# A hand-written list scheduler: longer planned load latency, a two-instruction LSTM cell, unbroken sums and an earlier rank for two batches

## The chip, the cores and the metric

The kernel runs on one core of one Trainium2 chip. The metric is the device time in microseconds, and the number that counts is the median of several executions. One further execution was profiled; its rows give start and duration of every instruction on the five engines: PE (TensorE, with PEld for its weight loads), DVE (VectorE), ACT (ScalarE), POOL (GpSimd) and SP (which here only issues DMAs).

## The reference, cut to what matters

There are 32 graphs ("batches") of 512 nodes with 128 features each, and an adjacency matrix of 512 x 512 of zeros and ones per graph. Four layers follow each other, each as `x = x + layer(relu(layernorm(x)), adj)`:

```
layer 0   attention:  q, k, v = relu(h Wq), relu(h Wk), relu(h Wv);  x += softmax(masked q k^T) v
layer 1   dyn  = conv1d(last 128 nodes of h)           # 32 x 128 steps x 128
          lw   = lstm(dyn)                             # 128 steps, for 32 graphs at once
          x   += sigmoid((D^-1/2 (A + I) D^-1/2 h) lw)
layer 2   four sublayers, each: tanh of (normalised A times projected nodes) + own projection
layer 3   x += prelu(A (h W^T) + bias)

lstm step:  z = dyn_t W_ih + b + h W_hh;   i, f, g, o = split(z)
            c = sigmoid(f) c + sigmoid(i) tanh(g);   h = sigmoid(o) tanh(c)
```

The LSTM needs only the last 128 nodes of each graph, but of all 32 graphs, so layer 0 must have been done for those nodes everywhere before step 0. Layer 1's result needs the LSTM's last state for every graph.

## The kernel before, in words

The fast path, `symmetric`, has four parts.

*Pass 1* (`pass_1`) does, for each batch, layer 0 for the last 128 nodes and the convolution, and stores keys, values and the normalised input in DRAM.

*The recurrence* (`lstm`) has 128 steps. A step is one block of small products on PE (L1216, tiles of 32 columns, "tiled"), a tanh of three gates on ACT (L1242), the cell on DVE (L1249 to L1251), a tanh of the fourth gate (L1257) and of the cell (L1259) on ACT, and the new state with its transpose on DVE (L1263, L1264). The transpose releases the next step's products. The sigmoids are written as tanh of half the argument, which is why the cell reads "(tanh + 1) times".

*Pass 2* (`pass_2`) does layer 0 for the other 384 nodes: it loads what pass 1 stored and the adjacency (L1284 to L1297), computes the query product (L1299), the scores (L1308), the exponentials times mask (L1311, L1312) and the weighted values (L1317), all with 32-column tiles on PE. `squares` (L1356) turns the adjacency into the type that PE takes and sums its rows, on ACT. For the first 24 batches (`EARLY`) it also does layer 1's sum over neighbours, `sums_of_1`, whose matmuls are in `aggregate` (L1403): two halves (high and low part of the values) of four matmuls 128x512 with 128x128 weights, each half an operation of its own. The updated x goes to DRAM (L1328), the sums too (L1344).

*The last stage* (`rest`) finishes layers 1 to 3 batch by batch: gates (L1452), the comparison of the adjacency with its transpose by two scans per batch on DVE (L1471), four sublayers (L1498 projection, L1385 and L1386 split into two parts, L1403 sum, L1505 scaling, L1509 own projection, L1513 tanh) and layer 3. It begins with batches 26 and 27 (`FIRST`).

All of these only record operations. `Plan.run` then decides the order on each engine: it simulates the engines with a duration given for each operation, a hop between engines, and for a DMA a `gap`, the extra time from the end of its issue slot to its landing (2.0 us if nothing else is said; the slot of 1024 KB is 0.1 + 1024/315 us). At each moment it takes the operation that can start first, and among those that can start at once the one of lowest rank. The LSTM steps have ranks 0 to 127, which are urgent: an operation that isn't urgent is passed over when it would still run, by more than 0.15 us, at the time at which the next urgent one is expected on its engine. Pass 1 has ranks from 10,000, pass 2 from 20,000, the last stage from 30,000; ranks of the last stage are recomputed from how much work lies behind an operation. The last four batches of pass 2 rank among the last stage. The order that comes out is fixed in the program: each engine executes its list in order and waits on semaphores, so an operation whose data come late holds all that stands behind it on its engine.

Buffers are named by tags with counts (`BUFS`); the whole adjacency has two buffers (`a`), the transformed one six (`ar`).

## Time and profile before

| | |
|---|---|
| median of 3 runs | 1316.08 us (1315.48 to 1326.4) |
| the profiled execution | 1324.53 us, span of its instructions 1322.7 us |
| PE, PEld busy | 1274.2 us (96%), 977.1 us (74%) |
| DVE, ACT, POOL busy | 990.9 us (75%), 847.3 us (64%), 392.8 us (30%) |
| first products of the recurrence, last transpose | about 182 us, about 515 us |
| mean DMA rate | 177 GB/s |

The shares are means over stages of different kinds. The stage from 182 to 515 us is the recurrence with pass 2 beside it; up to about 195 us pass 1 overlaps it; from 515 us the last stage runs alone, with what pass 2 has left. In a row of the profile, "x16" counts hardware instructions, of which one product in 32-bit floats takes two.

### The profile page before, as it was taken

Reading aid. Unit: us, or ns where it says so; the run is one execution under the profiler, and the core shown is the slowest. Engines: PE = TensorE matmul, PEld = TensorE weight load, DVE = VectorE, ACT = ScalarE, POOL = GpSimd, SP = SyncE. Lnnn points to the kernel's source line nnn. Section 1 sums busy time; section 2 is a strip of 40 time slices with the busy share of each in tenths; the row PEclk is TensorE's granted clock in tenths of the full one; section 3 lists DMA queues with packets and bytes.
Section 4 is the critical chain, followed back from the end, with each engine's and each line's share of the span. In section 5 each row is a group of like instructions: output and inputs, shape, how many; then the busy total and the mean of one; then the engine's idle time right before and its main releaser. Section 6 shows DMA issues by size and latency. Waiting matters only on the chain.

```text
span 1322.7 us, 32990 instructions
## 1 busy us (share of the span) xinstructions
PE 1274.2 (96%) x12098; PEld 977.1 (74%) x12099; DVE 990.9 (75%) x3392; ACT 847.3 (64%) x2116; POOL 392.8 (30%) x737
## 2 busy tenths in 40 slices
PE   9999999988988999799999999999999999999996
PEld 6888866656666667577787877778787787787774
DVE  7998878867868887766777767767677777787644
ACT  5666767666777665575666666666676676676423
POOL 4655432213213214422231322313223132242100
PEclk9999999999999999899999999999999999999999
DMA  8888888757757657895667766776767754673311
GB/s 259 261 284 276 266 292 260 238 170 225 230 185 238 202 164 217 194 211 145 158 142 159 165 156 160 158 152 161 154 163 160 166 124 88 151 170 71 48 33 35
DMA packets 300587, 234.52 MB, mean 177 GB/s; under 512 B 138240, under 2 KB 244480, under 8 KB 300416
## 3 DMA queue, kind: packets, MB, share of 16 engines
q1 hardware_dynamic: 283520, 215.54, 58.3%
q0 software_dynamic: 16896, 16.78, 8.1%
q8 instruction: 98, 1.61, 0.5%
q14 instruction: 73, 0.60, 0.2%
HBM read 138.16 MB, written 62.65 MB: 152 GB/s over the span
## 4 chain that ended last, share of the span: by engine, by line
PE 84%; DMA 5%; DVE 5%; ACT 2%; issue 2%; POOL 1%; SPq 1%; ACTq 0%; POOLq 0%; DVEq 0%
PE f_pa L1403 18%; PE f_py L1498 15%; PE f_pa L1509 15%; PE f_pg L1403 8%; PE f_s L1308 5%; PE f_po L1317 4%; PE f_z L1216 3%; DMA f_a<-in_adj_dram 3%; PE f_p L1550 2%; PE f_pl L1452 2%; PE f_pk L1123 2%; PE f_pv L1139 2%; PE f_sl L1156 2%; PE f_pol L1166 2%; PE f_pq L1299 1%
## 5 line engine op out<-in xcount | busy, mean ns | idle before, releaser
L1403 PE MATMUL f_pa<-f_ar,f_y 128*128 128x512 f32 x1024 | 300.5, 430 | 5.3 <-DVE f_y L1386 4.5
L1403 PEld LDWEIGHTS f_pa<-f_ar,f_y 128*128 128x128 f32 x1024 | 190.1, 189 | 80.5 <-issue 40.2
L1498 PE MATMUL f_py<-f_wf,f_n 128*128 128x128 f32 x1280 | 174.6, 275 | 0.8 <-ACT f_n L1513 0.8
L1498 PEld LDWEIGHTS f_py<-f_wf,f_n 128*128 128x128 f32 x1280 | 165.5, 192 | 11.2 <-ACT f_n L1513 1.9
L1509 PE MATMUL f_pa<-f_n,f_wf 128*128 128x512 f32 x320 | 152.8, 592 | 0.0
L1356 ACT ACTIVATE f_ar<-f_a 128x512 fp32r<-128x512 f32 x224 | 138.6, 621 | 19.5 <-DMA f_a<-in_adj_dram 18.3
L1513 ACT ACTIVATE f_n<-f_pa,f_bcol 128x512 f32<-128x512 f32 x128 | 88.3, 690 | 92.1 <-PE f_pa L1509 91.7
L1385 ACT CAST f_y<-f_py 128x512 fp32r<-128x512 f32 x128 | 75.0, 586 | 101.0 <-PE f_py L1498 98.7
L1466 POOL DMA_DIRECT2D f_das<-f_ar x32 | 26.9, 839 | 366.5 <-ACT f_ar L1356 313.4
L1317 PE MATMUL f_po<-f_v,f_e 128*32 128x129 f32 x3072 | 108.5, 277 | 8.3 <-issue 6.1
L1505 DVE TENSOR_TENSOR f_pa<-f_pa,f_inv 128x512 f32<-128x512 f32 x128 | 86.7, 693 | 30.6 <-PE f_pa L1403 30.2
L1317 PEld LDWEIGHTS f_po<-f_v,f_e 128*32 128x32 f32 x3072 | 91.0, 111 | 20.8 <-issue 10.4
L1386 DVE TENSOR_TENSOR f_y<-f_py,f_y 128x512 fp32r<-128x512 f32 x128 | 87.6, 685 | 22.7 <-ACT f_y L1385 22.6
L1308 PE MATMUL f_s<-f_q,f_k 128*32 128x384 f32 x1024 | 99.8, 488 | 0.1
L1216 PE MATMUL f_z<-f_w,f_seq 128*32 128x128 f32 x2040 | 83.2, 276 | 16.0 <-DVE f_seq L1264 8.1
L1216 PEld LDWEIGHTS f_z<-f_w,f_seq 128*32 128x32 f32 x2040 | 54.9, 109 | 56.0 <-issue 13.8
L1509 PEld LDWEIGHTS f_pa<-f_n,f_wf 128*128 128x128 f32 x320 | 57.5, 190 | 44.9 <-issue 37.6
L1471 DVE SCALAR_TENSOR_TENSOR f_junk<-f_a,f_aT 128x1024 bf16<-128x1024 f32 x64 | 78.1, 1220 | 5.5 <-DMA f_aT<-f_das 4.3
L1403 PE MATMUL f_pg<-f_ar,f_xp_d 128*128 128x512 f32 x256 | 74.4, 413 | 0.3 <-DVE f_xp_d L1394 0.2
L1498 PE MATMUL f_py<-f_wf,f_T_c 128*128 128x128 f32 x448 | 72.9, 275 | 0.0
L1078 DVE COPY f_hl_d<-f_n 128x1024 uint16<-128x1024 uint16 x28 | 19.4, 693 | 71.2 <-ACT f_n L1513 71.2
L1403 PE MATMUL f_pg<-f_ar,f_xp_c 128*128 128x512 f32 x256 | 71.9, 413 | 0.7 <-ACT f_x L856 0.7
(204 smaller groups left out, 2775.1 us busy)
## 6 DMA issues: line engine op xcount, KB each, us to landing
f_a<-in_adj_dram SPq DMA_DIRECT2D x56, 1024.0 KB
f_das<-f_ar POOLq DMA_DIRECT2D x32, 512.0 KB, 4.8
f_dkq<-f_kh SPq DMA_DIRECT2D x32, 448.0 KB
f_dv<-f_v SPq DMA_DIRECT2D x32, 258.0 KB
f_v<-f_dv SPq DMA_DIRECT2D x32, 258.0 KB
f_x<-in_x_dram SPq DMA_DIRECT2D x32, 256.0 KB
f_al<-in_adj_dram SPq DMA_DIRECT2D x32, 256.0 KB
f_k<-f_dkq SPq DMA_DIRECT2D x32, 256.0 KB
```

The source lines that it names most:

```text
L1216: nc.tensor.matmul(z.t[part, k, :, :], h, w[:, m : m + 4, part], start=False, stop=True, skip_group_check=True)
L1308: PE(R, t_mm(NR), lambda s=s, j=j: quarters(lambda p: nc.tensor.matmul(s.t[p], keys.t[:, j * P + p.start : j * P + p.stop], q.t, start=Tru ...
L1317: PE(R, t_mm(P), lambda t=t, j=j: quarters(lambda p: nc.tensor.matmul(po.t[p, t, :], es[j].t[:, t * P + p.start : t * P + p.stop], v.t[:, ...
L1356: ACT(rank, 0.62, lambda t=t: nc.scalar.activation(ar.t[:, t, :], a.t[:, t, :], AF.Square, accum_out=deg.t[:, t : t + 1]), [a], [(ar, t), ...
L1385: ACT(rank, t_act(N), lambda: nc.scalar.copy(parts.t[:, :, 0, :], src.t), [src], [(parts, 0)])
L1386: DVE(rank, t_dve(N), lambda: nc.vector.tensor_sub(parts.t[:, :, 1, :], src.t, f32(parts.t[:, :, 0, :])), [src, (parts, 0)], [(parts, 1)])
L1403: nc.tensor.matmul(pg.t, parts.t[:, j, k, :], ar.t[:, j, :], start=(k == 0 and j == 0), stop=(k == 1 and j == NT - 1))
L1471: nc.vector.scalar_tensor_tensor(junk, flat(a.t[:, 2 * k : 2 * k + 2, :]), 1.0, flat(aT.t[:, 2 * k : 2 * k + 2, :]), OP.mult, OP.not_equal ...
L1498: nc.tensor.matmul(py.t[:, j, :], nodes[n].t[:, bass.ts(j, P)], wf[:, W_F[i] + c, 0, :], start=False, stop=(c == nch - 1), skip_group_chec ...
L1505: before = DVE(R, t_dve(N), lambda pa=pa: nc.vector.tensor_mul(pa.t, pa.t, inv_row.t), [inv_row], [pa])
L1509: nc.tensor.matmul(pa.t, wf[:, W_F[i] + c, 1, :], nodes[n].t, start=False, stop=(c == nch - 1), skip_group_check=True)
L1513: ACT(R, 0.57, lambda pa=pa, n=n, i=i: nc.scalar.activation(n.t, pa.t, AF.Tanh, bias=bcol[:, i : i + 1]), [pa], [n])
```

## The change

It has four parts.

- *Loads.* The six loads of a batch in pass 2 get `gap=LANDED`, 3.8 us, in place of 2.0. Nothing about the transfers themselves is different; only the planner's idea of when they land.
- *Cell.* The cell state is no longer a tile of its own. It is written into slot 3 of the next step's gate tile, which gets five slots of 32: i, f, g, c, o. One instruction over two slots computes (i + 1) g and (f + 1) c; a second adds half of the latter. Before there were three instructions. The planner's duration goes from 0.43 to 0.30.
- *Unbroken sums.* For ranks below 30,000 `aggregate` is one operation of eight matmuls instead of two of four. It waits for both parts of the values, and it may overrun the next urgent operation by 1.3 us (`patience`), where the rest keeps 0.15.
- *Rank.* The first two batches of the last stage (all of their operations except the transposed copy, its scans, and what has its own rank) are ranked 9,950 lower, among pass 2.

```diff
@@ class Plan
+        self.soon = 0.0
...
+        o.patience = 0.15
...
-                o.rank = self.last + 12 * k - 9 * max(0, k - 28) + 200.0 - (min(behind[o], 60) if sub == 5 else behind[o] + (70 if sub == 2 else 0.0))
+                soon = self.soon if k < 2 and sub < 2 else 0.0
+                o.rank = self.last - soon + 12 * k - 9 * max(0, k - 28) + 200.0 - (min(behind[o], 60) if sub == 5 else behind[o] + (70 if sub == 2 else 0.0))
...
-                    elif held is not None and s < held < s + o.engines[e][0] - 0.15:
+                    elif held is not None and s < held < s + o.engines[e][0] - o.patience:
                         continue
...
+    SOON = 9_950.0
+    LANDED = 3.8
+    PATIENCE = 1.3
+    plan_rest = 30_000
@@ lstm
-            th = new("th", (P, 4, TURN), f"f_th_{t}")
+            th, after_th = after_th or new("th", (P, 5, TURN), f"f_th_{t}"), new("th", (P, 5, TURN), f"f_th_{t + 1}")
...
-            cn = new("c", (P, TURN), f"f_c_{t}")
+            cn = after_th
...
-                    nc.vector.scalar_tensor_tensor(u.t, th.t[:, 1, :], 1.0, c.t, OP.add, OP.mult)
-                    nc.vector.scalar_tensor_tensor(v.t, th.t[:, 0, :], 1.0, th.t[:, 2, :], OP.add, OP.mult)
-                    nc.vector.scalar_tensor_tensor(cn.t, u.t, 0.5, v.t, OP.mult, OP.add)
-                DVE(R, 0.43, cell, [(th, 0), c], [u, v, cn])
+                    nc.vector.scalar_tensor_tensor(uv.t, th.t[:, 0:2, :], 1.0, th.t[:, 2:4, :], OP.add, OP.mult)
+                    nc.vector.scalar_tensor_tensor(cn.t[:, 3, :], uv.t[:, 1, :], 0.5, uv.t[:, 0, :], OP.mult, OP.add)
+                DVE(R, 0.3, cell, [(th, 0), (th, 2)], [uv, (cn, 2)])
...
@@ pass_2 (all six loads alike)
-        DMA(R, 192, lambda: nc.sync.dma_start(hT.t, dkq.t[:, N:]), [dkq], [hT])
+        DMA(R, 192, lambda: nc.sync.dma_start(hT.t, dkq.t[:, N:]), [dkq], [hT], gap=LANDED)
...
@@ aggregate
+        def half(k):
+            for j in range(NT):
+                nc.tensor.matmul(pg.t, parts.t[:, j, k, :], ar.t[:, j, :], start=(k == 0 and j == 0),
+                                 stop=(k == 1 and j == NT - 1))
+
+        def both():
+            half(0)
+            half(1)
+        if rank < plan_rest:
+            last = PE(rank, 8 * t_r(N), both, [parts, ar], [pg])
+            last.patience = PATIENCE
+            return last
         for k in range(2):
...
-            last = PE(rank, 4 * t_r(N), fn, [(parts, k), ar], [pg])
+            last = PE(rank, 4 * t_r(N), lambda k=k: half(k), [(parts, k), ar], [pg])
         return last
@@ end of symmetric
-    plan.last, plan.spared = 30_000, 20_000
+    plan.last, plan.spared, plan.soon = 30_000, 20_000, SOON
```

Both programs have the same instructions except for one DVE instruction less in each of 127 steps (the cell), a matmul less that only marks a bank, and some work for which the planner may choose between ACT and DVE.

## The prediction

> **What bounds the kernel now.** I read the windows of the three stages around the change, then ACT's waits, then the timeline of one recurrence step with and without a stall, then the start of the last stage. First the windows (engine busy us and number of instructions, TensorE clock, DMA share, GB/s):

> ```profile
> 182.00:515.00 333.00, 307.06 (x6212) 213.62 (x6206) 266.49 (x1208) 238.19 (x833) 89.10 (x167) 0.99 0.68 213
> 515.00:560.00 45.00, 37.17 (x426) 28.58 (x424) 30.46 (x101) 19.79 (x50) 15.91 (x27) 0.92 0.88 221
> 560.00:667.00 107.00, 106.75 (x587) 83.81 (x588) 74.37 (x188) 70.15 (x155) 29.50 (x47) 1.00 0.72 169
> ```

> The 128 recurrence steps run from 182 to 515; there PE has 26 us idle, in the next 45 us 8, and from 560 none: afterwards PE's work alone sets the time. In the order of the instructions of both programs PE's last 2351 of about 6990 are the same, from 667 us on. So the change must win or lose before 667, and what it wins is PE's idle time and PE latency that counts as busy. ACT's waits from 182 to 515 (total, times, longest):

> ```profile
> ACT f_th L1242 <- PE f_z L1216: 41.5, 70, 2.6
> ACT f_tcn L1259 <- DVE f_c L1251: 21.4, 58, 0.7
> ACT f_ar L1356 <- DMA f_a<-in_adj_dram: 11.0, 7, 3.3
> ACT f_x L1050 <- DMA f_dx<-f_x: 4.5, 3, 2.7
> ```

> The third row is the harmful one. A step without a stall, then one with it (start, duration):

> ```profile
> 311.87 0.65 PE L1216 MATMUL f_z<-f_w,f_seq 128*32 128x128 f32 x16
> 312.36 0.25 ACT L1242 ACTIVATE f_th<-f_z 128x96 f32<-128x96 f32 x1 [0.22 <-PE f_z L1216]
> 312.64 0.19 DVE L1249 SCALAR_TENSOR_TENSOR f_cu<-f_th,f_c 128x32 f32<-128x32 f32 x1
> 312.75 0.19 DVE L1250 SCALAR_TENSOR_TENSOR f_cv<-f_th 128x32 f32<-128x32 f32 x1
> 312.98 0.19 DVE L1251 SCALAR_TENSOR_TENSOR f_c<-f_cu,f_cv 128x32 f32<-128x32 f32 x1
> 313.03 0.58 SPq L1287 DMA_DIRECT2D f_a<-in_adj_dram  x1
> 313.26 0.23 ACT L1259 ACTIVATE f_tcn<-f_c 128x32 f32<-128x32 f32 x1
> 313.82 0.21 DVE L1264 STREAM_TRANSPOSE f_seq<-f_h 128x32 f32<-128x32 f32 x1
> ...
> 321.16 0.63 ACT L1356 ACTIVATE f_ar<-f_a 128x512 fp32r<-128x512 f32 x1 [2.76 <-DMA f_a<-in_adj_dram]
> 322.40 0.23 ACT L1242 ACTIVATE f_th<-f_z 128x96 f32<-128x96 f32 x1
> 322.66 0.19 DVE L1249 SCALAR_TENSOR_TENSOR f_cu<-f_th,f_c 128x32 f32<-128x32 f32 x1 [2.55 <-ACT f_th L1242]
> ```

> The next step's products start at 314.18: 2.31 us a step. At 321 ACT stands before a square whose adjacency has not landed, and the step's tanh is queued behind it. This load was issued at 313.03 and landed at 321.16: 8.1 us; the planner reckons 3.35 + 2.0 = 5.35. Over the 128 steps the mean is 2.60 us, the median 2.40. Start of the last stage:

> ```profile
> 544.69 1.23 DVE L1471 SCALAR_TENSOR_TENSOR f_junk<-f_a,f_aT 128x1024 bf16<-128x1024 f32 x1
> 545.85 0.69 DVE L1386 TENSOR_TENSOR f_y<-f_py,f_y 128x512 fp32r<-128x512 f32 x1
> 546.59 2.08 PE L1403 MATMUL f_pa<-f_ar,f_y 128*128 128x512 f32 x4 [4.50 <-DVE f_y L1386]
> ```

> PE waits 4.5 us, since pass 2 is used up and nothing else is ready.

> [...] The trace shows no time of its own for that: at 312.44 a 128x128 sum starts while the 128x32 products of the step, recorded to 312.52, are not over, and the gaps after such sums are ended by the step's transpose. I price a change of mode at nothing, at most 0.1 us.

> **The change, part by part.**
> *Cell.* Before, three instructions take 0.34 + 0.19 = 0.53 us, mean 0.517. [...] Saved 0.075 a step, at most 127 x 0.075 = 9.5 us, but only where the chain, not PE, sets the step. To size this I gave each gap between two steps, in both orders, its PE work, at increments taken from the timeline (24 records of L1308 last 2.15 us, 16 last 1.50, and so on): four products of L1308 or L1299 0.645, of L1317 0.22, a step 0.44 (0.22 without the look-ahead products), a sum matmul of L1403 0.232, a matmul of the weight folding 0.22 (its transposes 0.11). Per gap I took the larger of this and the chain (2.25 before, 2.17 after). Before: 294.8 us over 125 gaps, with the first two at 2.35 299.5. After: 301.1 over 127 gaps at 2.25, 295.2 at 2.17. So the new order costs 1.6 and the cell returns 5.9: -4.3.
> *Unbroken sums.* Eight matmuls are 1.86 us, as long as the 1.8 left beside a step's products. In the order 24 blocks lie inside the recurrence (before 42 half blocks and 3 whole ones after it). Mode changes hardly fall inside the recurrence (90 to 86), so no gain is taken for these. Nine blocks share their gap with other work and overrun by 0.8 to 1.0; that is in the 301.1. Work left after the last step: before 132 L1317, 16 L1308 and 24 sum matmuls, 7.3 + 2.6 + 5.6 = 15.5; after 152 L1317, 8.4. Of the 7.1 gained, 2.0 is moved ahead of the first step (12 L1317, 4 L1308, 4 L1299), where PE is full: -5.1.
> *Loads.* Planned at 3.35 + 3.8 = 7.15, the adjacency loads are 1 us short of what I measured instead of 2.8. In SP's order several of them now stand ahead of loads of x, which wait for a store (49 us in all for L1294). That store's wait stays, and so do PE's own gaps of 2.0 us put down to issue (three). Of the 11.0 us ACT wait I let 2 remain and add 2 for PE work queued behind the late steps (the step at 401.6 took 4.07): -11, bounds 0 and -14. The five other loads of a batch move likewise and wait for nobody on the path. POOL keeps its 747 instructions.
> *Rank.* The first two batches of the last stage go ahead of the rest of pass 2, whose 152 products then fill the gaps of their chain. But DVE still has two scans of L1471 (2.5 us), waiting for a transposed copy, ahead of the product of L1505. Of the 8 us I take -3, bounds 0 and -7. If this cover fails, what is late next is the same f_y.
> Sum: -4.3 - 5.1 - 11 - 3 = -23.4 against this execution's 1324.5 (span 1322.7 and 1.8 around it): 1301. The execution is 8.4 over the median of 1316.1; I assume that about half of that is stalls which the change removes: 1296. A measurement of this kernel can tell about 1%, or 13 us, from no change.

> **Rivals.**
> *The stalls stay* (0.20): loads take still longer when they come earlier, as SP and DMA do no less work. For it: 8.1 exceeds 7.15, and x loads still block SP. Against: two adjacency buffers leave time. Then -4.3 - 5.1 - 3 = -12.4: 1312 on the scale of this execution, 1308 with the same 4 off for the median.
> *The gain is given back* (0.12): the recurrence ends sooner, but the last stage starts just as empty, with scans before f_y, and PE gaps of issue and of stores grow. A gain of 4 against the median: 1312.
> *Unbroken blocks hold the recurrence* (0.10): once a step is late, the block in front of it on PE is too. With 1.3 us of allowed overrun for each of 24 blocks, 31 us; from 1.0 us each it eats the whole gain. With the loads unmended 31 - 12.4 = +19 to the median: 1335. For it: after the stall at 397 a step waited for 2.88 us of queued PE work. Against: whole blocks already among the halves of before passed in 2.24 to 2.30 us.
> *The forecast* (0.58): 1284 to 1306.

> **Numbers.** Faster by over 1% (below 1303): 0.58 x 0.92 + 0.20 x 0.25 + 0.12 x 0.15 = 0.60; slower by over 1% (above 1329): 0.10; the rest 0.30. The range, 1282 to 1314, takes in the bounds of the loads and the first two rivals.

> **What would show it.** Right: the last step ends near 500, the median step is 2.30 or less, ACT waits for the adjacency under 4 us in the recurrence, PE idle from there to the full stretch is under 6, and from the common order on nothing changes. Wrong: steps of 3 us or more behind sums of eight, or ACT's wait for DMA still at 10.

## The result, and the profile after

The changed kernel takes 1317.51 us in the median of 20 executions (1309.55 to 1326.79), the kernel before 1321.68 us on the same chips (1315.48 to 1329.29). The ratio is 0.9972, 95% interval 0.995 to 0.9995: a gain of 4 us where 20 was forecast. The profiled execution took 1317.18 us, 7.3 us less than that of before.

First the page of the kernel after: busy us of each engine, share of the span, instructions.

```profile
span 1315.4 us, 32850 instructions
...
PE 1275.1 (97%) x12097; PEld 974.1 (74%) x12098; DVE 992.6 (75%) x3286; ACT 833.2 (63%) x2095; POOL 392.4 (30%) x737
```

PE's busy time is that of before (1274.2) to 0.9 us. In this pair of executions what the change won is PE's idle time, span minus busy: 48.5 us before, 40.3 after. This subtraction is the key to the case, so each experiment below is told with it. Now the three windows that answer to the ones shown of before (width, busy time of each engine with its number of instructions, clock, DMA share, GB/s):

```profile
184.00:523.40 339.40, 315.22 (x6193) 215.47 (x6194) 265.17 (x1090) 230.78 (x817) 87.30 (x163) 0.98 0.68 212
523.40:560.00 36.60, 35.81 (x439) 28.81 (x438) 33.40 (x110) 18.79 (x50) 17.25 (x28) 1.00 0.95 228
560.00:673.00 113.00, 111.68 (x604) 86.24 (x602) 81.02 (x213) 72.01 (x161) 31.21 (x52) 1.00 0.78 179
```

The recurrence became 6 us longer (337 from the first tanh to the last transpose, 331 before), and PE's idle time in it is still 24 us (26 before). Behind it PE is nearly full: 0.8 and 1.3 idle in the second and third window, where 7.8 and 0.3 were. From the common order on (667.1 us before, 660.7 after; the third window reaches a little into it) PE's last 646.1 us are equal to 0.1 us in both. ACT's waits in the recurrence (total, times, longest), the four that were shown of before:

```profile
ACT f_th L1249 <- PE f_z L1223: 44.1, 68, 4.5
...
ACT f_tcn L1263 <- DVE f_th L1256: 21.2, 46, 0.6
...
ACT f_x L1057 <- DMA f_dx<-f_x: 5.8, 3, 2.1
...
ACT f_ar L1360 <- DMA f_a<-in_adj_dram: 2.4, 3, 0.9
```

The last row fell from 11.0 to 2.4 us: the loads do arrive in time. The row above it, the wait for the store of x (the pass writes over x in the same buffer once it is stored), did not fall (4.5 before); with VectorE's own wait for that store it is 12.9 us after and 10.1 before. The first row shows that the steps wait for PE as long as before. From the timeline of all engines, an ordinary step, and one with a block of eight in front of the next step's products (start, duration, engine, line, operation):

```profile
502.98 0.65 PE L1223 MATMUL f_z<-f_w,f_seq 128*32 128x128 f32 x16
...
503.47 0.25 ACT L1249 ACTIVATE f_th<-f_z 128x96 f32<-128x96 f32 x1
...
503.75 0.22 DVE L1255 SCALAR_TENSOR_TENSOR f_cu<-f_th 128x64 f32<-128x64 f32 x1 [0.83 <-ACT f_th L1249]
...
504.01 0.19 DVE L1256 SCALAR_TENSOR_TENSOR f_th<-f_cu 128x32 f32<-128x32 f32 x1
...
504.30 0.23 ACT L1263 ACTIVATE f_tcn<-f_th 128x32 f32<-128x32 f32 x1 [0.49 <-DVE f_th L1256]
...
504.79 0.21 DVE L1268 STREAM_TRANSPOSE f_seq<-f_h 128x32 f32<-128x32 f32 x1
...
506.37 2.14 PE L1406 MATMUL f_pg<-f_ar,f_xp_c 128*128 128x512 f32 x8
...
507.02 0.21 DVE L1268 STREAM_TRANSPOSE f_seq<-f_h 128x32 f32<-128x32 f32 x1
...
508.43 0.38 PEld L1223 LDWEIGHTS f_z<-f_w,f_seq 128*32 128x32 f32 x16 [0.36 <-issue]
```

The new cell takes 0.45 us (0.517 before; mean 0.449). In the second step the transpose ends at 507.23 and the next weights are loaded at 508.43: PE had its block to finish. Over all steps the time from transpose to products rose from 33.6 to 49.9 us. PE works in most of that time (it is idle for 10.3 of the 49.9 us, 7.8 of the 33.6), so most of it costs the step and not the kernel. At the start of the last stage, in the timeline of PE alone, value products of pass 2 (L1321) stand where PE waited 4.5 us:

```profile
541.31 1.18 PE L1406 MATMUL f_pa<-f_ar,f_y 128*128 128x512 f32 x4
542.42 2.20 PE L1321 MATMUL f_po<-f_v,f_e 128*32 128x129 f32 x72
544.55 1.12 PE L1521 MATMUL f_pa<-f_hT_c,f_wf 128*128 128x512 f32 x2
```

Last, the longest gap of PE in the recurrence, in the timeline of PE alone, and the windows around it:

```profile
425.72 0.48 PE L1312 MATMUL f_s<-f_q,f_k 128*32 128x384 f32 x1
429.71 0.86 PE L1312 MATMUL f_s<-f_q,f_k 128*32 128x384 f32 x4 [3.51 <-issue]
```
```profile
425.00:428.00 3.00, 1.20 (x25) 0.55 (x17) 2.37 (x10) 1.06 (x4) 0.00 (x0) 1.00 0.89 259
428.00:431.00 3.00, 1.29 (x13) 0.77 (x16) 0.00 (x0) 0.00 (x0) 0.00 (x0) 0.64 0.34 118
431.00:434.00 3.00, 3.00 (x35) 1.58 (x31) 1.88 (x9) 1.49 (x5) 1.20 (x3) 0.50 0.00 2
434.00:437.00 3.00, 3.00 (x62) 2.47 (x58) 1.64 (x8) 1.61 (x6) 0.57 (x2) 0.72 0.00 0
437.00:440.00 3.00, 3.00 (x105) 2.68 (x102) 2.79 (x11) 2.25 (x7) 0.00 (x0) 1.00 0.57 163
```

PE stops between two products of the same group, with no wait that the profile shows, for 3.51 us; its clock is granted at half for 6.8 us, from 428.9 on, and the record of a score product lasts 0.85 instead of 0.48 us. The step in which this falls took 6.83 us, the longest of all. Gaps of this kind decide much of what follows. Those over 1 us came to 6.3 us before (three) and 10.4 after (four).

### The profile page after: what moved, and what is told of

Its sections match the earlier page's. It is cut to its first block, busy times and chain, and to the rows that moved or that the text cites. A ratio compares the mean times of both kernels' runs of the same rounds, so it can differ in the third digit from the quotient of the medians.

```text
span 1315.4 us, 32850 instructions
## 1 busy us (share of the span) xinstructions
PE 1275.1 (97%) x12097; PEld 974.1 (74%) x12098; DVE 992.6 (75%) x3286; ACT 833.2 (63%) x2095; POOL 392.4 (30%) x737
## 4 chain that ended last, share of the span: by engine, by line
PE 84%; DVE 6%; DMA 4%; ACT 3%; issue 2%; POOL 1%; SPq 0%; ACTq 0%; DVEq 0%; POOLq 0%
PE f_pa L1406 17%; PE f_py L1510 15%; PE f_pa L1521 14%; PE f_pg L1406 9%; PE f_s L1312 4%; PE f_z L1223 4%; PE f_po L1321 4%; PE f_p L1562 2%; PE f_pol L1173 2%; PE f_pk L1130 2%; PE f_pv L1146 2%; PE f_pl L1464 2%; PE f_sl L1163 2%; DMA f_a<-in_adj_dram 2%; PE f_pd L1198 1%
## 5 line engine op out<-in xcount | busy, mean ns | idle before, releaser
L1312 PE MATMUL f_s<-f_q,f_k 128*32 128x384 f32 x1024 | 106.6, 500 | 6.4 <-issue 5.7
L1321 PE MATMUL f_po<-f_v,f_e 128*32 128x129 f32 x3072 | 108.6, 273 | 4.3 <-issue 4.2
L1321 PEld LDWEIGHTS f_po<-f_v,f_e 128*32 128x32 f32 x3072 | 90.7, 110 | 22.8 <-issue 14.2
L1223 PE MATMUL f_z<-f_w,f_seq 128*32 128x128 f32 x2040 | 87.0, 280 | 13.0 <-DVE f_seq L1268 5.9
L1315 ACT ACTIVATE f_e<-f_s 128x384 f32<-128x384 f32 x128 | 61.5, 484 | 26.0 <-PE f_s L1312 14.1
```

Source lines behind the costliest of these rows:

```text
L1223: nc.tensor.matmul(z.t[part, k, :, :], h, w[:, m : m + 4, part], start=False, stop=True, skip_group_check=True)
L1312: PE(R, t_mm(NR), lambda s=s, j=j: quarters(lambda p: nc.tensor.matmul(s.t[p], keys.t[:, j * P + p.start : j * P + p.stop], q.t, start=Tru ...
L1321: PE(R, t_mm(P), lambda t=t, j=j: quarters(lambda p: nc.tensor.matmul(po.t[p, t, :], es[j].t[:, t * P + p.start : t * P + p.stop], v.t[:, ...
```

## The experiments

Us against before are (ratio - 1) x 1321.7; the changed kernel has -3.7 on this scale. Idle is span minus PE's busy time on the page. "Issue" is the sum of PE's gaps over 1 us put down to issue in the recurrence. "Half clock" is the time between 20 and 700 us at a granted clock of 0.5. The last four columns are of one execution each.

| kernel | ratio to before [95%] | us | PE busy | idle | issue | half clock |
|---|---|---|---|---|---|---|
| before | | 0 | 1274.2 | 48.5 | 6.3 | 13.7 |
| changed | 0.9972 [0.995, 0.9995] | -3.7 | 1275.1 | 40.3 | 10.4 | 10.2 |
| e1 unbroken sums alone | 0.9974 [0.9957, 0.9991] | -3.4 | 1273.8 | 53.5 | 11.3 | 20.5 |
| e2 loads alone | 0.9978 [0.9963, 0.9994] | -2.9 | 1272.6 | 44.1 | 7.5 | 10.2 |
| e3 cell alone | 1.0095 [1.0068, 1.0123] | +12.6 | 1277.2 | 51.0 | 2.4 | 23.9 |
| e4 rank alone | 1.0012 [0.9989, 1.0035] | +1.6 | 1278.1 | 49.9 | 5.2 | 13.7 |
| e5 changed, short cell | 0.9899 [0.9874, 0.9923] | -13.3 | 1270.6 | 37.8 | 10.3 | 10.2 |
| e6 changed, sums in halves | 1.0066 [1.0044, 1.0089] | +8.7 | 1282.1 | 46.9 | 6.4 | 17.1 |
| e7 changed, old cell | 1.0011 [0.9996, 1.0026] | +1.5 | 1275.2 | 44.3 | 8.0 | 20.5 |
| e8 changed again | (one execution) | | 1273.9 | 45.2 | 11.7 | 13.7 |
| e9 new cell, order of before | 0.9972 [0.9954, 0.9989] | -3.7 | 1276.2 | 43.1 | 5.1 | 23.9 |
| e10 changed, cell planned 0.43 | 1.0029 [1.0011, 1.0046] | +3.8 | 1281.0 | 50.1 | 10.3 | 34.1 |
| e11 changed, without rank | 1.0021 [1.0004, 1.0039] | +2.8 | 1278.8 | 45.2 | 12.4 | 20.5 |
| e12 changed, old load times | 1.0105 [1.0081, 1.013] | +13.9 | 1278.2 | 51.7 | 2.0 | 13.7 |
| e13 changed, more traffic | 1.0037 [1.0014, 1.006] | +4.9 | 1276.0 | 45.7 | 9.7 | 10.2 |
| e14 before again | (one execution) | | 1275.0 | 51.8 | 6.5 | 17.1 |
| e15 changed, later stores | 0.9915 [0.9886, 0.9943] | -11.2 | 1270.9 | 39.3 | 9.0 | 10.2 |
| e16 changed, cell planned 0.36 | 1.0027 [1.0011, 1.0042] | +3.6 | 1275.5 | 41.4 | 4.1 | 20.5 |
| e19 changed, less traffic | 0.9909 [0.9874, 0.9944] | -12.0 | 1268.0 | 30.9 | 2.0 | 0.0 |
| e20 before, later stores | 1.0011 [0.9992, 1.0031] | +1.5 | 1274.8 | 43.2 | 4.0 | 23.9 |

One execution of a kernel can lie 10 us from its median: of e1 and e10 the slowest of all was profiled, of e3, e16 and e19 the fastest. e8 and e14 give the scatter of the two kernels compared.

### Each part alone

```diff
 e1, on before                              e2, on before: LANDED = 3.8
+        if rank < plan_rest:               -  ... [dkq], [hT])
+            last = PE(..., both, ...)      +  ... [dkq], [hT], gap=LANDED)
+            last.patience = PATIENCE       (and the five other loads)
```

> The kernel before with the sums of eight and their patience of 1.3 us as the only part of the change. Theory A (the blocks overrun into the steps): the time from a step's transpose to the next step's products grows as it did in the whole change, by 10 us or more over the 128 steps (it was 33.6 us in all before, 49.9 after), the last step ends 6 to 15 us later than before, and the time is +2 to +12. Rival B (the blocks are harmless, and what was lost came from PE's own gaps of 2 to 3.5 us, which fall where they fall): that sum stays within 5 us of before, the time is -5 to +2 (less work left after the last step), and steps that come late stand beside gaps put down to issue.

> The kernel before with the loads of the second pass planned 1.8 us later as the only part. As the prediction had it: ACT's wait for the adjacency in the recurrence falls from 11 to under 4 us and the time by 8 to 12. Theory A: the same fall of the wait, and at least half of it in the time (-5 to -12), since no block of eight eats it. Rival C (the stall was hidden or is replaced: a step that ACT holds up lets PE catch up on its queue): the wait falls, and the time changes by less than 3.

e1: the time from transpose to products rose to 50.0 us and the last step ended at 532, 17 us later, as theory A had it; yet the kernel became 3.4 us faster, which only rival B allowed. A step that waits behind a block is late, but the block would have been PE's work anyway. Rival B was right in the time and wrong in the mechanism: its sum within 5 us of before did not come.

e2: ACT's wait for the adjacency fell from 11.0 to 3.1 us; the time fell by 2.9, as rival C had it. The wait was not hidden, but replaced. In the kernel before, three of ACT's stalls opened a gap of PE. One is the stall at 321 that the prediction shows (PE's gap: 2.41 us). The others, where the step's tanh, or a product's mask, stands behind the late square:

```profile
292.94 0.63 ACT L1356 ACTIVATE f_ar<-f_a 128x512 fp32r<-128x512 f32 x1 [2.54 <-DMA f_a<-in_adj_dram]
293.57 0.21 ACT L1259 ACTIVATE f_tcn<-f_c 128x32 f32<-128x32 f32 x1
...
294.31 0.65 PE L1216 MATMUL f_z<-f_w,f_seq 128*32 128x128 f32 x16 [1.98 <-DVE f_seq L1264]
...
393.00 0.63 ACT L1356 ACTIVATE f_ar<-f_a 128x512 fp32r<-128x512 f32 x1 [3.29 <-DMA f_a<-in_adj_dram]
...
394.93 0.43 PE L1317 MATMUL f_po<-f_v,f_e 128*32 128x129 f32 x8 [2.04 <-DVE f_e L1312]
```

Together 6.4 us of PE (5.8 in e14). In e2 they are gone; but the waits of ACT and VectorE for the store of x rose from 10.1 to 18.4 us, and behind two of these waits PE stood still again:

```profile
DVE f_x L1054 <- DMA f_dx<-f_x: 12.8, 8, 4.3
...
ACT f_x L1057 <- DMA f_dx<-f_x: 5.6, 4, 3.5
```
```profile
373.83 0.64 PE L1223 MATMUL f_z<-f_w,f_seq 128*32 128x128 f32 x16 [3.08 <-DVE f_rinv L1328]
...
387.22 0.64 PE L1223 MATMUL f_z<-f_w,f_seq 128*32 128x128 f32 x16 [2.55 <-DVE f_seq L1271]
```

```diff
 e3, on before                                     e4, on before
-  scalar_tensor_tensor(u.t, th.t[:, 1, :], ...)   -  plan.last, plan.spared = 30_000, 20_000
-  scalar_tensor_tensor(v.t, th.t[:, 0, :], ...)   +  plan.last, plan.spared, plan.soon = 30_000, 20_000, SOON
+  scalar_tensor_tensor(uv.t, th.t[:, 0:2, :], ...)
-  DVE(R, 0.43, cell, ...)
+  DVE(R, 0.3, cell, ...)
```

> The kernel before with the cell in two instructions as the only part. The prediction's working: 0.07 us less in each of 127 cells (0.517 to 0.449 as in the whole change), of which about 6 us reach the end of the recurrence: -4 to -7. Rival C (PE's queue sets most steps): cell as short, time within 3 of before.

> The kernel before with only the first two batches of the last stage ranked ahead. PE's order is the same as before up to about the end of the recurrence, so the recurrence keeps its length within the scatter of one execution (some 5 us); PE's idle time after it falls from 8.1 to about 2, and the time by 4 to 6 (the whole change showed 5.8 less idle there). If the idle time falls but the time does not, the gap has come back later.

e3: the cell is as short as forecast (0.451), and the recurrence 13 us shorter. The kernel is 12.6 us slower. Its order leaves 64 score products, 12 query products and 228 value products behind the last step (before: 16, none and 132), the time from the last transpose to VectorE's last instruction grows from 800.0 to 818.5 us, and in the last stage PE stands still once for long (timeline of PE alone, start and duration):

```profile
535.46 2.84 PE L1464 MATMUL f_pl<-f_lw,f_gT 128*128 128x128 f32 x24
546.04 0.73 PE L858 MATMUL f_xt_c<-f_ident,f_xn_c 128*128 128x128 f32 x2 [7.73 <-DVE f_xn_c L1054]
```

From about 542 us on, within this gap, the clock is granted at half for 13.7 us. e4: PE's idle time behind the recurrence did not fall (10.1 us, before 8.1): the early gap went, and one of 3.53 us came at 584.6, ahead of a projection that waits for a tanh on ACT. The gap was moved.

### One part taken back, and the chain itself

```diff
 e5, on changed
-  scalar_tensor_tensor(uv.t, th.t[:, 0:2, :], 1.0, th.t[:, 2:4, :], OP.add, OP.mult)
-  scalar_tensor_tensor(cn.t[:, 3, :], uv.t[:, 1, :], 0.5, uv.t[:, 0, :], OP.mult, OP.add)
+  scalar_tensor_tensor(cn.t[:, 3, :], th.t[:, 0, :], 1.0, th.t[:, 2, :], OP.add, OP.mult)
 e6: plan_rest = -1      e7: the cell of before, planned at 0.43
```

> The changed kernel with the same order of instructions on every engine, the cell cut to one VectorE instruction of 32 elements: the forget gate's part of the cell (old state times forget gate) is left out. It takes some 0.25 us out of the chain of each of 127 steps, 32 us in all. Theory P (PE's work sets the time; the chain only matters where PE runs dry before a step's products): the gaps of under 1.2 us that the step's transpose ends, some 6 us, go and the time falls by 3 to 8. Theory Q (the chain of the step sets the time, as the prediction's cell term of 5.9 us from 0.075 a step had it): it falls by 15 to 25.

> The changed kernel with the early sums in two halves again, all else as changed. Theory A (the sums of eight hold the steps up): the time from a step's transpose to the next products falls from 49.9 to about 34 us and the recurrence by 10 or more. Theory P: a shorter recurrence leaves the same PE work to be done behind it (about 21 score products and 72 of the value products instead of 38), so the time changes only by what PE's idle time changes: within 5 of the changed kernel, and PE's busy time up to the common order is again 640 to 646 us.

> The changed kernel with the three-instruction cell of before, all else as changed. Alone, the new cell made the kernel about 10 us slower, although the recurrence ended 13 us sooner. If what it cost there is the work that it leaves to the start of the last stage, then here, where only 12 value products are left over, the old cell is as good as the new one or better: -6 to +2 against the changed kernel. As the prediction had it: +6.

> The changed kernel unaltered, one more profiled execution, to see which of PE's gaps are part of the program and which of the execution. If the gaps put down to issue (2.16 us at 221.5, 3.07 at 332.0, 1.69 at 394.5, 3.51 at 429.7) are chance, they lie elsewhere or have other lengths; if they are tied to a place in PE's instructions, they come back at the same instructions with 1 to 4 us each.

e5 took 127 x (0.449 - 0.189) = 33 us out of the chain of the steps, at the same order, and won 9.6 us against the changed kernel, a little more than theory P's 8 and below Q's 15 to 25. PE sets the time; here a microsecond of chain was worth 0.3.

e6: theory A fell altogether. The steps are on time again (27.2 us from transpose to products), the recurrence is 25 us shorter, and the kernel is 12.4 us slower than the changed one. Theory P failed as well: it allowed 5 us, and no more work of PE, but PE is busy for 1282.1 us against 1275.1. One term of that is seen in the timeline. A block of eight sums in the changed kernel, a half in e6:

```profile
506.37 2.14 PE L1406 MATMUL f_pg<-f_ar,f_xp_c 128*128 128x512 f32 x8
```
```profile
455.72 1.20 PE L1406 MATMUL f_pg<-f_ar,f_xp_c 128*128 128x512 f32 x4
```

Two halves are 2.40 us. By the records of single products the first after 32-column products ends 0.43 us after the product before it, each of the others 0.23 (medians): 0.2 for each change of mode, some 39 entries against 25, 3 us. The rest of the 7 us of busy time belongs partly to the half clock (17.1 us against 10.2).

e7: without the new cell +5.2 against the changed kernel, so here the cell is worth about what was forecast, although alone it cost 12.6. e8: of the gaps put down to issue, those at 332 and at 394 came back at the same instructions (3.43 and 1.15 us), one at 221 came back with 1.19; the longest, at 430, did not, and one of 3.15 at 288 was new. So the place is fixed, and whether PE stops there is chance. In every run each such gap over 1 us from 20 us on, 76 in all, lies at instruction 192 to 194 past a multiple of 256 in PE's list (8385 = 32 x 256 + 193, and so on).

### Why the parts do not add

```diff
 e9 (before with the new cell), e10 (changed):      e11: SOON = 0.0     e12: LANDED = 2.0
-  DVE(R, 0.3, cell, ...)
+  DVE(R, 0.43, cell, ...)
```

> The kernel before with the cell in two instructions, but planned at the 0.43 us of before, so that the order of instructions on PE is exactly that of before. It parts the two halves of the cell's effect when made alone (+10 us): the instructions and the new order that their shorter planned time brings (0.43 to 0.30 in the plan, 0.517 to 0.449 on the chip). Theory R (the order is the loss: a step planned shorter by more than it becomes shorter takes less other work beside it, and more is left for the start of the last stage): -2 to -5 against before, the recurrence 2 to 5 us shorter. Rival: if the instructions themselves lose (the state in the same buffer as the gates), no gain or +3 and more. As the prediction had it, -5.9.

> The changed kernel with the new cell planned at 0.43 us. The order on PE is then exactly that of the changed kernel without the new cell (e7), with only 48 value products left after the last step where the changed kernel has 152. Theory R: against e7, the instructions alone give -2 to -5, so 1318 to 1321; since e7's order and the changed kernel's lie 6 us apart by the time, this also says how much of those 6 is the order: near 1317, none; near 1321, some 4.

> The changed kernel without the first two batches ranked ahead. By PE's idle time behind the recurrence (7 to 10 us wherever the rank was not changed or stood alone, 2.1 and 6.1 in two executions of the changed kernel) it is 2 to 6 us slower than the changed kernel: 1319 to 1323. If the rank does nothing: 1316 to 1319.

> The changed kernel with the second pass's loads planned at 2.0 again. By the prediction's step (11 us of ACT's wait on the path) it is 9 to 12 us slower than the changed kernel: 1326 to 1330, with ACT's wait for the adjacency back at 8 or more. By PE's gaps (of the 11 us of ACT's wait in the kernel before only one gap of PE, 2.41 us, was ended by the square of a late adjacency) it is 2 to 4 slower: 1319 to 1322.

e9 is the clean measure of the two instructions: at the order of before, -3.7 us. So in e3 the order cost about 16. e10, at the order of e7, was not faster than e7 but 2.4 us slower (the intervals overlap), and 7.5 slower than the changed kernel, with 34.1 us at half clock in its profiled execution. Theory R, that the shorter planned time is what loses, is true of the kernel before and false of the changed one; I give it up as a rule. e11: +6.5 against the changed kernel, a little over the 2 to 6 expected. e12: +17.6, more than either expectation, though ACT's wait for the adjacency was only 3.7 us and one gap of PE, 2.34 us, came of it. The larger gaps, 4.76 us at 271 and 3.07 at 450, stand behind waits for the store of x (18.9 us of ACT and VectorE, 12.9 in the changed kernel), and PE's idle time behind the recurrence came to 10.6.

Alone the four parts sum to -3.4 - 2.9 + 12.6 + 1.6 = +7.9 us; taken out of the changed kernel one at a time they are worth 12.4, 17.6, 5.2 and 6.5. Each edit makes the planner write another order, from about the tenth step on at the latest (the rank's only in the last dozen steps). Where nothing but the cell's planned time differs, the order is all that differs, and it was worth 16 us (e3 against e9), 7.5 (changed against e10, the other way) and 7.3 (changed against e16). How much of each other number is the order's isn't shown.

### What the gaps are

```diff
 e13, with each adjacency load of pass 2
+            nc.sync.dma_start(copy, dkq.t[:, :N])        # DRAM to DRAM, 256 KB
 e19, the same loads (and t % 3, j % 3 where the tiles are read)
-            nc.sync.dma_start(a.t, adj[b] ...)
+            nc.sync.dma_start(a.t[:, :3, :], adj[b, : 3 * P] ...)
```

> The changed kernel with the same order on PE, and beside each adjacency load of the second pass one more copy of 256 KB from DRAM to DRAM that nobody reads. If PE's gaps at every 256th instruction come from instruction packets that arrive late because the DMA engines are full, they grow from the 10 to 12 us of the two executions of the changed kernel to 15 or more, at the same instructions (index 193 or 194 past a multiple of 256), each ending 1.3 to 1.5 us after a packet of 16 KB has landed, and the time rises by 5 to 20. If they have another cause, they stay at 8 to 13, and only waits for loads grow.

> The kernel before unaltered, one more profiled execution. The gaps at every 256th instruction come to 4 to 7 us again (6.3 in the first, 5.1 in e9 with the same order on PE) if the changed kernel's 10 to 12 belong to the change; to 8 or more if they are scatter. PE's idle time behind the recurrence: 8.1 in the first; 6 to 9 expected.

> The changed kernel with the same order on PE, the adjacency loads of the second pass cut by a quarter (the last of their four tiles is not read, the third is used twice; the two batches whose adjacency is used again later keep theirs). If late instruction packets are a matter of DMA traffic, PE's gaps at every 256th instruction fall from 12 us to under 8, and the time by 3 to 8. If traffic of this size is not what delays them, they stay at 10 to 13 and the time within 3 of the changed kernel.

e14 repeats the 6.3 us (6.5, and 5.1 in e9), so the changed kernel's 10.4 and 11.7 belong to its order. e13: the gaps did not grow (9.7), which is what was expected if DMA traffic is not their cause; what grew are the waits of ACT and VectorE for the store of x, 22.7 us against 12.9, and the kernel lost 8.6 us. e19: with a quarter less adjacency the gaps are 2.0 us, where the four other executions at this order (changed, e5, e8, e13) have 9.7 to 11.7, and the kernel gains 8.3 us against the changed one. In the profiled execution no half clock is left between 20 and 700 us. Its page, and its windows of the recurrence and behind it:

```profile
PE 1268.0 (98%) x12098; PEld 970.5 (75%) x12098; DVE 991.2 (76%) x3286; ACT 832.8 (64%) x2095; POOL 394.2 (30%) x737
```
```profile
182.00:504.50 322.50, 308.07 (x6190) 211.62 (x6193) 262.84 (x1087) 229.81 (x815) 89.40 (x164) 1.00 0.66 203
504.50:560.00 55.50, 53.98 (x553) 42.81 (x542) 47.46 (x149) 29.89 (x73) 21.20 (x34) 1.00 0.92 212
```

With the changed kernel's order unaltered the last transpose ends at 506, 17 us sooner and near what the prediction wrote ("near 500"), and PE's busy time is the lowest of all kernels. This is the fastest of six executions, though, 7.5 us under their median; over all six the mean granted clock was 0.996, where the 20 of the changed kernel have 0.994. So less DMA traffic went with shorter gaps; why more of it (e13) did not add to them is not settled. Nor is the share of this gain that the smaller loads brought by arriving sooner: the waits for the store of x fell to 6.8 us too.

### Later stores, and the plan of the cell between the two

```diff
 e15 (changed), e20 (before, gap=3.8)                         e16 (changed)
-  DMA(R + 5, 192, ... dx.t ..., [dx])                        -  DVE(R, 0.3, cell, ...)
+  DMA(R + 5, 192, ... dx.t ..., [dx], gap=LANDED)            +  DVE(R, 0.36, cell, ...)
```

> The changed kernel with the store of the second pass's x planned with 3.8 us of latency too. Waits of ACT and VectorE for this store fall from 13 to 15 us to under 5 in the recurrence. If they hold steps up as the prediction's step on the adjacency took for granted of ACT's waits, -5 to -8 against the changed kernel: 1310 to 1313. If PE has work queued during most of them, as in e2: 1315 to 1322, the scatter of a new order.

> The kernel before with the store of the second pass's x planned with 3.8 us of latency as the only edit. If what e15 gained (some 6 us against the changed kernel) belongs to the edit, -4 to -8 here too: 1313 to 1318, with the waits of ACT and VectorE for this store in the recurrence down from 10 to under 4 us. If it belongs to the order that it happened to bring, this one scatters by as much as the other new orders did: anything from -3 to +10.

> The changed kernel with the cell planned at 0.36 us, 0.07 less than before, which is what it becomes shorter on the chip, instead of 0.13 less. Only 56 value products are left after the last step instead of 152, and 304 sum products instead of 320 (9 us less of PE work). If filling the recurrence gains, 1308 to 1313. If PE's work is the same wherever it stands, and only its idle time counts: 1314 to 1322.

e15: the waits of ACT and VectorE for the store fell from 12.9 to 3.1 us, and the time by 7.5: 1311.65 us in the median, and its interval lies below that of the changed kernel. It is the fastest version here that computes everything. e20, the same edit on before: the waits fell from 10.1 to 5.4 us, the time not at all (0.9992 to 1.0031). The edit had less to win there: PE's gaps behind these waits (over 0.5 us, within 3.5 us after a wait of over 0.5) come to 0.7 us in the kernel before and 4.3 in e14, against 5.3 in the changed one and 7.5 in e8. In e15 they are 1.3, in e20 3.4. How much of e15's gain is the edit's and how much the order's is not settled. e16 leaves only 56 value products and came out 7.3 us slower than the changed kernel, above both expectations: less work left is not less work.

## Why the prediction was wrong, point by point

*The bound* was read right: PE, up to the common order, and nothing changed behind it. But the sum did not keep to it. PE's busy time is 1268 to 1282 us in all kernels, so the time is this plus PE's idle time. A step of the working could only count with the gap of PE that it closes or the work of PE that it saves.

*Cell and new order, -4.3.* The saving of 0.075 a step, an estimate made when no instruction of 64 elements was in a trace, measured 0.068. The instruction over 64 elements takes 225 ns (L1255, median), which the trace of before could have given: 192 for 32 elements (L1251) and 681 for 512 (L1394) put 64 at 225 on a straight line. What was mis-sized is how much of it is PE's: gaps of PE under 0.5 us ahead of a step's products, which a shorter chain can close, came to 6.2 us in all before and 4.4 after. e9 puts the instructions at -3.7 (forecast 5.9 of return). The price of the order, taken as +1.6 from a model of gaps, was mis-sized too, and has no one value: planning the cell at 0.30 instead of 0.43 cost about 16 in the kernel before (e3 against e9) and won 7.5 in the changed one (against e10).

*Unbroken sums, -5.1.* Alone -3.4. The reason given, less work left behind the last step, failed: the work went into a recurrence that grew by 6 us (e16, with still less left, lost). Two things were priced wrongly. The change of mode, taken at nothing, costs 0.2 us an entry (0.43 against 0.23 for a product); the prediction's own lines had it, for at 312.44 they let a sum of four start, whose record lasts 1.20 us where four products at its 0.232 are 0.93. And the blocks' overrun, the rival with +19, made steps late, but cost no time in e1 or against e6, since PE works meanwhile.

*Loads, -11.* The wait fell as forecast, to 2.4, and e2 measured -2.9. This is the largest error, 8 us, and two steps made it. The whole of ACT's wait was put on the path, where PE stood idle behind it for 6.4 us only. And "That store's wait stays" did not hold: in e2 it grew from 10.1 to 18.4 us, and PE's gaps behind it rose from 0.7 to 5.3 us in the changed kernel (4.3 to 7.5 in the second executions).

*Rank, -3.* In the changed kernel PE's idle time behind the recurrence fell from 8.1 to 2.1 us (8.9 to 6.1 in the second executions), which is 6.0 of the 8.2 us of idle time that the change won (2.8 of 6.6 in the second executions): with the other parts the term was met, and e11 puts it at 6.5. Alone the rank won nothing (e4).

*What was assumed to stay:* "so do PE's own gaps of 2.0 us put down to issue". They grew from 6.3 to 10.4 us (6.5 to 11.7). With the 3 to 5 us more behind the store this took back about what PE no longer stood behind late loads, so that its idle time in the recurrence fell by 2 us only. Of the rivals, "The gain is given back" had the size, a gain of 4, and this half of the mechanism, "PE gaps of issue and of stores grow"; the rest of it, a recurrence that ends sooner and an empty start of the last stage, did not come.

*The median.* Half of the 8.4 us between the profiled execution and the median of three was to be removable. The median of 20 is 1321.7, so that difference was 2.8 us in all, and the 5 taken off to reach 1296 had no ground. (It also reads POOL's 737 instructions as 747; nothing rests on that.)

## What to carry to other kernels

Where one engine sets the time, write the sum as its busy time plus its idle time, and let a step count only with the gaps of that engine that it closes; a wait on another engine is worth no more than the gap behind it. To find that gap, follow the wait through the engines: the releaser named at the gap is only the last link (VectorE's transpose at 294, behind ACT's late square). Then ask which wait comes next once this one is gone. Where a planner writes the order, an edit of a duration is two changes, and only a kernel that keeps the order (e5, e9, e13, e19) measures the first. An edit's worth on one order (e15) says little of its worth on another (e20).

## What the runs showed of the hardware

*Instruction packets.* Every gap of PE over 1 us put down to issue lies at the same place of a stretch of 256 instructions (192 to 194), and in the recurrence ends 1.2 to 1.6 us after a packet of 16 KB has landed on the instruction queue (q8 of the page). Ahead of the gap at 430 us that packet started 6.2 us after PE had passed the same place of the stretch before, where half of the 53 from 184 to 548 us start within 2.6. The page counts 97 such packets for the 24,533 records of PE's list, 253 to a packet (98 for 24,548 before). The gaps last 2.0 to 2.3 us in the kernel before, 1.7 to 3.5 in the changed one, and 1.0 to 5.3 over all runs. PE comes to the end of 256 instructions every 7 us in the recurrence. That the late packet is the cause of the gap is read from the place and the landing; no run delayed packets alone.
